# A two-layer graph kernel: weight rows over 128 partitions, a reordered start, and A h2 ahead of the last products

## Chip, cores and metric

The kernel runs on one core of a Trainium2 chip. The metric is the device time of one execution in microseconds (us), taken as the median of several runs; lower is better. The profile is one more execution, recorded by the hardware profiler; its own span is 2327.0 us.

## The reference

128 graphs of 128 nodes with 512 features. Layer 0 is a diffusion with an attention-weighted transition matrix; layer 1 is a linear attention over the adjacency matrix. Both take the layer norm and relu of their input and add to it. All is float32. In both, B = 128, N = 128, D = 512:

```
h  = relu(layernorm(x))
Xw = h @ Wv0 + bv
e  = leaky_relu(Xw @ aw[:d] (per column) + Xw @ aw[d:] (per row) + ab, 0.2)
T  = adj * exp(e), each row divided by its sum
x  = x + relu(h @ Wk[0] + bk[0] + T h @ Wk[1] + bk[1] + T T h @ Wk[2] + bk[2])

h2 = relu(layernorm(x))
q, k = split(h2 @ Wqk);  v = h2 @ Wv1
w  = (1 / sqrt(512)) * mask * rowsum(q * (adj @ (k * mask)))
x  = x + softmax over the nodes(w) * v
```

## The kernel before, in words

**Tiling.** Two graphs make a pair (p = 0 to 63), and one pair is worked on at a time. Nodes lie on the 128 partitions. The weights stay in SBUF for the whole run.

**The algebra.** Xw is never formed. `attention_columns` (L175) multiplies Wv0 by the two attention vectors into one extra column for each half of Wk[2], so that one product h [Wk[2] | column] gives Y2 and the attention terms together (257 columns for each half). T is then applied in two steps: Y10 + T (Y1 + T Y2), called `inner` (L426) and `outer` (L436). In layer 1 the score q * (A k) is computed as h2 M * (A h2) with M = Wq Wk^T, one 512x512 "score matrix" made at the start by `score_matrix` (L224) in four steps f = 0 to 3, so that one product h2 [M | Wv1] gives both the score side and v. A h2 is made by `aggregate` (L448), one 128x512 product for each graph.

**Strassen.** The products of a pair (2 graphs by 2 halves of the columns) use 7 block products in place of 8 (`strassen`, L306). It needs sums of the left side (`left_sums`, L294, on VectorE) and of the right side (`combine`, L156, on VectorE, once for each weight: `right2` for Y2, `right10` for Y10, `rightl` for layer 1). The seven products are issued in the order 1, 5, 6, 2, 7, 3, 4 into four PSUM banks a, e, b, c, with ScalarE copies between banks. There are two sets of banks: set 1 (a1, b1, c1, e1) for Y10, `inner`, `outer` and the score matrix; set 2 (a2, b2, c2, e2) for Y2 and layer 1. The argument `steps` lets other work be issued after a given product.

**Setup.** The input DMAs are issued by SP: x of pair 0 (L78), Wqk in four tiles (L117), Wv0, Wk[2], x of pair 1, Wk[1] and Wk[0] (all through `rows`, L136), later the adjacency (L84) and Wv1. `rows` permutes the rows of a weight: for each c it loads 32 partitions, each with four row pieces. Small constants come through the queues of ScalarE (L118) and GpSimd (L119 to L123). TensorE then transposes Wqk (`weights_transposed`, L209, eight groups of four transposes, each followed by a ScalarE copy) and h of pair 0 (`transposed_by_pe`, L286). The attention vectors are spread over the partitions by two products with a row of ones (L178) and two ScalarE copies (L179).

**Order.** Each engine works through its own queue in order. A scheduler sets the order of the queues from the order in which the code issues the work; `tc.issue_after(x)` says that what is issued within it stands after instruction x, and `behind` is a short form of that. In the loop, pair p runs Y10(p), the transpose of T (`t_transposed`, L395), `inner`, Y2 of pair p + 1, `outer`, then layer 1 of pair p - 1, and on the other engines the norm and transposes of the pairs ahead (`norm0`, `begin`, `norm2`, `attention`). For the transposes of h on VectorE, h goes to DRAM (`hd`) and comes back in blocks (`hv`). For pairs 0 and 1 the attention column is spread over the partitions by two TensorE transposes (`spread`, L152), for later pairs by DMA through GpSimd's queue. `seed` (L404) copies the bias into banks a1 and e1, into which Y10 accumulates.

**The end.** After the last pair's layer 0 only layer 1 of pair 63 remains (`layer1` with `last`). There, graph 0's A h2 follows product 3, its score and softmax follow at once (`score`, L499; `finish_graph`, L493), and graph 1's A h2 follows product 4. `end22` also finishes pair 62 (L538 scales its v and adds it to x).

Of the kernel before, what the change touches and what calls it, by code (L numbers as in the profile page):

```python
# [8 lines left out]
FP = mybir.dt.float32  # L9
# [6 lines left out]
def kernel(  # L16
# [30 lines left out]
    G = 2  # L47
# [19 lines left out]
                                      ("a1", "b1", "c1", "e1", "a2", "b2", "c2", "e2"))  # L67
    set1, set2 = (a1, b1, c1, e1), (a2, b2, c2, e2)

    def bcast(ap, offset, n):  # L70

        return bass.AP(tensor=ap.tensor, offset=ap.offset + offset, ap=[[0, P], [1, n]])
# [33 lines left out]
    wkt = setup.tile([P, DC, D], FP, name="wkt")  # L106
    aw_bc = setup.tile([P, 2, D], FP, name="aw_bc")
    awr = t10[0:1, 2].rearrange("p c o -> p (c o)")
    bkr = t10[:K, 3, 0]
    nm = setup.tile([B, N], FP, name="nm")  # L110
    ab_bc = setup.tile([P, 1], FP, name="ab_bc")
    awc = setup.tile([P, 2, DC], FP, name="awc")
# [22 lines left out]

    def rows(dst, w):  # L136

        for c in range(DC):
            nc.sync.dma_start(dst[c * S32:(c + 1) * S32],
                              w[c * P:(c + 1) * P].rearrange("(f a) o -> a f o", a=S32))  # L140

    def rows_by_halves(dst, w):
        for nh in range(2):
# [28 lines left out]
    maskT = const.tile([P, B], FP, name="maskT")  # L172
    wscale = const.tile([P, B], FP, name="wscale")

    def attention_columns():  # L175

        for a, bank in enumerate((b2, c2)):
            nc.tensor.matmul(bank, ones[0:1, :], awr[:, a * D:(a + 1) * D], start=True, stop=True)  # L178
            nc.scalar.copy(aw_bc[:, a, :], bank)  # L179
        for f in range(DC):  # L180
            for a in range(2):
                junk = front.tile([P, D], FP, name="junk", bufs=1)
                nc.vector.scalar_tensor_tensor(junk, wv0_sb[:, f], 1.0, aw_bc[:, a, :], op0=OP.mult,
                                               op1=OP.mult, accum_out=r2[:, f, a, HD:W2])

    def attention_constant():

        ccol = small.tile([P, 2], FP, name="ccol", bufs=1)
        for a in range(2):
            nc.vector.scalar_tensor_tensor(awc[:, a], awc[:, a], 1.0, bvc, op0=OP.mult,  # L190
                                           op1=OP.mult, accum_out=ccol[:, a:a + 1])
        for a in range(2):
            nc.tensor.matmul(e2[:, 0:1], ones, ccol[:, a:a + 1], start=(a == 0), stop=(a == 1))
        nc.vector.tensor_add(cz, e2[:, 0:1], ab_bc)

    def masks():

        nc.tensor.transpose(a2[:, :B], nm, ident[:B, :B])
        nc.scalar.copy(maskT, a2[:, :B])
        nc.scalar.activation(wscale, maskT, AF.Copy, scale=float(D) ** -0.5)  # L200

    def bias():


        nc.tensor.matmul(b2, ones[:K, :], bkr, start=True, stop=True)
        nc.scalar.copy(bias_a[:, 1], b2[:, :HD])
        nc.vector.tensor_sub(bias_e[:, 1], b2[:, HD:], bias_a[:, 1])

    def weights_transposed():  # L209

        banks = [a2, e2, a1, b1, c1, e1]
        for c in range(DC):
            for a in range(2):
                bank = banks[(c * 2 + a) % len(banks)]
                pt = bank.rearrange("p (o i) -> p o i", o=DC)
                for o in range(DC):
                    at = a * D + o * P
                    nc.tensor.transpose(pt[:, o, :], wqk_sb[:, c, at:at + P], ident)
                if a:
                    nc.scalar.copy(wkt[:, :, c * P:(c + 1) * P], pt)  # L220
                else:
                    nc.scalar.copy(wqt[:, :, :, c, :], pt.rearrange("p o (f a) -> p o f a", f=Q))

    def score_matrix(f):  # L224

        bank = set1[f]
        for o in range(DC):
            nc.tensor.matmul(bank, wqt[:, o, f].rearrange("p c a -> p (c a)"), wkt[:, o],
                             start=(o == 0), stop=(o == DC - 1))
        nc.scalar.copy(rl[:, f, :, 0, :], bank.rearrange("p (h o) -> p h o", h=2))  # L230


# [73 lines left out]
    def strassen(banks, left, right, s, first, ends, steps={}):  # L306

        w = right[1].shape[-1]  # L310
        a, b, c, e = (t[:, :w] for t in banks)

        def product(bank, i, start=False):
            for k in range(HC):
                nc.tensor.matmul(bank, left[i][:, k * P:(k + 1) * P], right[i][:, k],  # L315
                                 start=(start and k == 0), stop=(k == HC - 1),
                                 skip_group_check=True)
            if i in steps:
                steps[i]()

        product(a, 1, first)
        nc.scalar.copy(b, a)  # L322
        product(e, 5, first)
        nc.scalar.copy(s[:, 0], e)  # L324
        product(b, 6)
        done["u2"] = nc.scalar.copy(c, b).ins  # L326
        product(a, 2)
        ends[0, 0](a)
        product(c, 7)
        nc.scalar.copy(s[:, 1], c)  # L330
        ends[1, 1](e, s[:, 1])
        product(b, 3)
        ends[0, 1](b, s[:, 0])
        product(c, 4)
        ends[1, 0](c)
# [11 lines left out]
    def y2(p):  # L347

        y = Y2[p] = front.tile([P, G, 2, WP], FP, name="y2")[:, :, :, :W2]
        s = front.tile([P, 2, WP], FP, name="s2", bufs=1)[:, :, :W2]  # L350
        strassen(set2, LEFT[p], right2, s, True, {
            (0, 0): lambda a: nc.scalar.copy(y[:, 0, 0], a),
            (1, 1): lambda e, t: nc.vector.tensor_add(y[:, 1, 1], e, t),  # L353
            (0, 1): lambda b, t: nc.vector.tensor_add(y[:, 0, 1], b, t),
            (1, 0): lambda c: nc.scalar.copy(y[:, 1, 0], c)})
        if p > 1:

            t = small.tile([P, G, S32], FP, name="pzt", bufs=1)
            nc.vector.transpose(t, y[:, :, 0, W2 - S32:])  # L359
            d = dram.tile([G, Q, S32], FP, name="pzd")  # L360
            nc.gpsimd.dma_start(d.rearrange("g q b -> q g b"), t[S32 - 1::S32])  # L361
            PZ[p] = front.tile([P, G, N], FP, name="pz", bufs=1)
            nc.gpsimd.dma_start(PZ[p].rearrange("p g n -> p (g n)"), bcast(d, 0, G * N))
        else:
            PZ[p] = a2[:, :G * N].rearrange("p (g n) -> p g n", g=G)
            for j in range(G):
                spread(PZ[p][:, j, :], y[:, j, 0, HD:])
        return s

    def attention(p, room):  # L370

# [29 lines left out]
        nc.scalar.copy(tt, pt)  # L401
        TT[p] = tt

    def seed():  # L404

        nc.scalar.copy(a1, bias_a.rearrange("p k o -> p (k o)"))
        nc.scalar.copy(e1, bias_e.rearrange("p k o -> p (k o)"))

    blocks1 = [(0, 0, a1), (1, 1, e1), (0, 1, b1), (1, 0, c1)]

    def behind(what, op, *args):

        with tc.issue_after(done[what]):
            return op(*args)

    def y10(p, steps):

# [37 lines left out]
    def layer1(p, steps={}):  # L455
# [10 lines left out]

        def end12(b, t):
            nc.vector.tensor_add(o[0, 1], b, t)
            aggregate(p, 0, a2)
            if last:  # L470
                score(p, yv, w, a2, 0)
                finish_graph(p, yv, w, 0, b1)

        def end22(e, t):
            nc.vector.tensor_add(o[1, 1], e, t)
            if last:
                end(t[:, :G])

        strassen(set2, LEFT2.pop(p), rightl, s, True, {
            (0, 0): lambda a: nc.scalar.copy(o[0, 0], a),  # L480
            (1, 1): end22,
            (0, 1): end12,
            (1, 0): lambda c: nc.scalar.copy(o[1, 0], c)}, steps)
        aggregate(p, 1, e2)
        if last:
            score(p, yv, w, e2, 1)
            finish_graph(p, yv, w, 1, c1)
        else:
            score(p, yv, w, a2, 0)
            score(p, yv, w, e2, 1)  # L490
        return yv, w, s
# [54 lines left out]
            finish(peak, *ends.pop())  # L546


    h0 = norm_relu(xg[0], "h", front, True)
    weights_transposed()  # L550
    hT0 = front.tile([P, G, DC, N], FP, name="x")
    transposed_by_pe(h0, hT0, (a2, e2))
    attention_columns()
    attention_constant()
    bias()
    LEFT[0] = left_sums(hT0, front, "sx", 2)
    score_matrix(0)
    score_matrix(1)
    masks()
    right2 = combine(halves(r2), [t2[:, i] for i in range(4)])  # L560
    with tc.issue_after(done["right"]):
        norm0(1)
    right10 = combine(halves(r10), [t10[:, i] for i in range(4)])
    with tc.issue_after(done["right"]), tc.issue_after(done["hv"]):
        for p in range(2):
            load_adj(p)
        y2(0)
        attention(0, front.tile([P, D], FP, name="junk", bufs=1)[:, :G * N])
        load_x(2)
        load_adj(2)  # L570
        rows_by_halves(rl[:, :, :, 1, :], wv1)
    score_matrix(2)
    score_matrix(3)
    seed()

    HV2 = {}
    for p in range(NP + 1):
# [5 lines left out]
        if p < NP:  # L583
# [10 lines left out]
                transposed(HV2.pop(p - 1), X2)  # L594
                LEFT2[p - 1] = left_sums(X2, late["p"], "sx2", 1)

            s0 = y10(p, {1: lefts, 6: lambda: t_transposed(p)})
            z = inner(p)
            s2 = y2(p + 1) if p + 1 < NP else s0
            end(s2[:, 0, :G])  # L600
            outer(p, z)
            if p == 0:
                setup_ctx.close()
                late["p"] = ctx.enter_context(tc.tile_pool(name="late", bufs=1))
            if p + 1 < NP:
                seed()
            if p == 0:
                norm2()
            if p + 3 < NP:
# [46 lines left out]
```

## Time and profile before

| what | value |
|---|---|
| median of 3 runs | 2328.38 us (2328.36 to 2328.64) |
| span of the profiled execution | 2327.0 us |
| TensorE (PE) busy | 2304.2 us, 99% |
| VectorE (DVE) busy | 1361.0 us, 58% |
| ScalarE (ACT) busy | 1028.8 us, 44% |
| GpSimd (POOL) busy | 336.6 us, 14% |
| mean granted clock of PE | 0.999 |
| share of the chain that ended last on PE | 98% |
| DMA | 241.55 MB, mean 104 GB/s; SP's and ACT's queue 29.9% of the 16 DMA engines' time, GpSimd's 5.1% |

PE is TensorE's matmuls, PEld its weight loads, SP the engine that issues most DMAs. "L218" is line 218 of the kernel before. A float32 product of a 128x512 tile appears as two MATMUL records of 0.43 us each when the clock is up, so "x8" is four products. A transpose is one record. In the tile names the buffer and bank numbers are left out: "a" is a1 or a2, "t" can be t2, t10 or the T of the attention. "[7.14 <-ACT aw_bc L179]" says that the engine stood idle for 7.14 us before this instruction, until ACT had written aw_bc at L179. The granted clock in the tables is the throttle's, not the start-up state of PE; that one shows in the durations.

### The profile page before, as it was taken

The numbers are of one execution on the slowest core, as the hardware profiler recorded it, in microseconds if no ns is written. First come the engines' busy times: TensorE is split into PE (matmuls) and PEld (weight loads), VectorE is DVE, ScalarE is ACT, GpSimd is POOL, SyncE is SP. The second block draws the span as 40 slices with busy tenths as digits, with TensorE's granted clock in tenths as the row PEclk, the third lists the DMA queues.
The fourth block names the chain that finished last, engine by engine and source line by source line (L and its number), as shares of the span: only waits on it lengthen the run. The fifth ranks groups of instructions, "written<-read, shape, count | busy, mean of one in ns | idle before, by whom it ended". The sixth has DMA issues, their size and how long they took to land.

```text
span 2327.0 us, 23621 instructions
## 1 busy us (share of the span) xinstructions
PE 2304.2 (99%) x6881; PEld 1290.7 (55%) x6881; DVE 1361.0 (58%) x4131; ACT 1028.8 (44%) x2517; POOL 336.6 (14%) x585
## 2 busy tenths in 40 slices
PE   7999999999999999999999999999999999999998
PEld 4555555555555555555555555555555555555554
DVE  3656566556556565565665665665656655656654
ACT  3444444444444444444444444444444444444443
POOL 2111111111111111111111111111111111111100
PEclk9999999999999999999999999999999999999999
DMA  7433333333333333333333333333333333333321
GB/s 171 113 105 98 121 89 106 111 98 109 103 102 110 105 97 114 97 98 114 95 109 110 99 108 103 98 114 105 90 118 91 108 111 98 109 102 99 109 64 50
DMA packets 249860, 241.55 MB, mean 104 GB/s; under 512 B 26062, under 2 KB 175566, under 8 KB 249730
## 3 DMA queue, kind: packets, MB, share of 16 engines
q1 hardware_dynamic: 229360, 215.01, 29.9%
q0 software_dynamic: 20368, 25.03, 5.1%
q8 instruction: 54, 0.88, 0.2%
q14 instruction: 76, 0.62, 0.1%
q10 hardware_dynamic: 2, 0.00, 0.0%
HBM read 140.20 MB, written 99.74 MB: 103 GB/s over the span
## 4 chain that ended last, share of the span: by engine, by line
PE 98%; ACT 1%; DVE 0%; DMA 0%; issue 0%; POOL 0%; DVEq 0%; ACTq 0%; POOLq 0%
PE a L315 24%; PE c L315 24%; PE b L315 24%; PE e L315 12%; PE a L453 2%; PE e L453 2%; PE a L431 1%; PE c L431 1%; PE c L441 1%; PE b L441 1%; PE e L431 1%; PE e L441 1%; PE b L431 1%; PE a L441 1%; PE a L400 1%; ACT h L257 0%
## 5 line engine op out<-in xcount | busy, mean ns | idle before, releaser
L315 PE MATMUL a<-r,x 128*128 128x257 f32 (+1 forms) x1024 | 373.1, 486 | 1.4 <-ACT b L322 1.4
L88 POOL DMA_DIRECT2D agb<-in_adj_dram x256 | 152.2, 599 | 844.7 <-DVE t L386 783.2
L353 DVE TENSOR_TENSOR y<-e,s 128x257 f32<-128x257 f32 x64 | 27.3, 427 | 403.8 <-ACT s L330 403.8
L315 PEld LDWEIGHTS a<-r,x 128*128 128x128 f32 x1024 | 189.3, 190 | 107.3 <-issue 91.2
L315 PE MATMUL a<-rl,x 128*128 128x512 f32 x512 | 240.7, 592 | 1.4 <-issue 1.4
L330 ACT COPY s<-c 128x512 f32<-128x512 f32 (+1 forms) x192 | 97.8, 510 | 209.5 <-PE c L315 209.4
L315 PE MATMUL c<-t,sx 128*128 128x257 f32 (+1 forms) x512 | 186.6, 487 | 1.2 <-ACT c L326 1.1
L315 PE MATMUL c<-t,x 128*128 128x257 f32 (+1 forms) x512 | 186.3, 486 | 0.3 <-ACT s L330 0.3
L315 PE MATMUL e<-t,sx 128*128 128x257 f32 (+1 forms) x512 | 186.4, 486 | 0.0
L315 PE MATMUL b<-t,sx 128*128 128x257 f32 (+1 forms) x512 | 186.2, 486 | 0.0
L315 PE MATMUL b<-r,sx 128*128 128x257 f32 (+1 forms) x512 | 186.2, 486 | 0.0
L361 POOL DMA_DIRECT2D pzd<-pzt x62 | 36.9, 595 | 951.5 <-DVE pzt L359 905.9
L326 ACT COPY c<-b 128x512 f32<-128x512 f32 (+1 forms) x192 | 95.8, 499 | 177.4 <-PE b L315 177.4
L324 ACT COPY s<-e 128x512 f32<-128x512 f32 (+1 forms) x192 | 98.8, 515 | 161.8 <-PE e L315 161.7
L283 DVE STREAM_TRANSPOSE x<-hv 128x512 f32<-128x512 f32 x252 | 163.5, 686 | 6.1 <-DMA hv<-hd 6.0
L315 PEld LDWEIGHTS a<-rl,x 128*128 128x128 f32 x512 | 97.2, 190 | 96.9 <-issue 93.6
L246 DVE TENSOR_TENSOR r<-r 128x2 f32<-128x2 f32 x128 | 20.0, 156 | 211.1 <-ACT r L245 210.9
L322 ACT COPY b<-a 128x512 f32<-128x512 f32 (+1 forms) x192 | 96.1, 500 | 97.7 <-PE a L315 89.7
L315 PEld LDWEIGHTS c<-t,sx 128*128 128x128 f32 x512 | 96.9, 190 | 70.6 <-issue 60.5
L315 PEld LDWEIGHTS c<-t,x 128*128 128x128 f32 x512 | 97.2, 190 | 68.7 <-issue 61.2
L315 PEld LDWEIGHTS b<-r,sx 128*128 128x128 f32 x512 | 97.3, 190 | 68.1 <-issue 61.2
L315 PEld LDWEIGHTS b<-t,sx 128*128 128x128 f32 x512 | 97.3, 190 | 68.1 <-issue 45.9
(205 smaller groups left out, 3910.2 us busy)
## 6 DMA issues: line engine op xcount, KB each, us to landing
hd<-h SPq DMA_DIRECT2D x126, 512.0 KB, 2.8
hv<-hd SPq DMA_DIRECT2D x504, 128.0 KB, 2.9
xg<-in_x_dram SPq DMA_DIRECT2D x64, 512.0 KB, 3.9
out_dram<-x SPq DMA_DIRECT2D x63, 512.0 KB, 4.3
agb<-in_adj_dram POOLq DMA_DIRECT2D x256, 32.0 KB, 2.1
ag<-in_adj_dram SPq DMA_DIRECT2D x64, 128.0 KB, 2.6
pw<-pwd POOLq DMA_DIRECT2D x63, 128.0 KB, 3.4
pz<-pzd POOLq DMA_DIRECT2D x62, 128.0 KB, 3.7
```

The lines of the kernel that those rows point to most:

```text
L88: nc.gpsimd.dma_start(agb[p][c * S32:(c + 1) * S32].rearrange("p g q i -> p (g q) i"), v[c])
L283: nc.vector.transpose(dst[:, j].rearrange("p f (n b) -> p f n b", n=Q), hv[:, j].rearrange("p n (f a) -> p f n a", f=Q))
L315: nc.tensor.matmul(bank, left[i][:, k * P:(k + 1) * P], right[i][:, k], start=(start and k == 0), stop=(k == HC - 1), skip_group_check=True)
L322: nc.scalar.copy(b, a)
L324: nc.scalar.copy(s[:, 0], e)
L326: done["u2"] = nc.scalar.copy(c, b).ins
L330: nc.scalar.copy(s[:, 1], c)
L353: (1, 1): lambda e, t: nc.vector.tensor_add(y[:, 1, 1], e, t),
L361: nc.gpsimd.dma_start(d.rearrange("g q b -> q g b"), t[S32 - 1::S32])
L431: nc.tensor.matmul(bank[:, :HD], TT[p][:, j, :], y[:, j, nh, :HD], start=False, stop=True, skip_group_check=True)
L441: nc.tensor.matmul(bank[:, HD:], tt[:, j, :], z[:, j, nh], start=False, stop=True, skip_group_check=True)
L453: nc.tensor.matmul(to, AT[p][:, j, :], h2, start=True, stop=True)
```

## The change

1. `rows` loads each weight in four DMAs over all 128 partitions, one row piece for each partition, in place of four DMAs over 32 partitions with four pieces each. Bytes, number of DMAs and placement in SBUF stay.
2. The bias rows `bkr` get a tile of their own (they lay in t10), and the small setup products use other banks (e1, c1).
3. Four products of `ones` with itself (`warm(4)`) stand first on TensorE, then the two attention vectors (`attention_vectors`, split off), then six more (`warm(6)`); the norm of pair 0 and the transposes of Wqk come behind them. Half of the copies after Wqk's transposes go to VectorE.
4. Three steps of the score matrix stand ahead of Y2 of pair 0, the fourth behind it; `combine` for `right10`, and `attention(0)`, come ahead of `norm0(1)`; the adjacency of pairs 0 and 1 is loaded ahead of h's way through DRAM. `seed` is split into `seed_a` and `seed_e`; the spreading of the attention column is split off Y2 (`spread_columns`).
5. In the loop, `t_transposed` is issued behind product 6, and pair 1's attention column is spread right after Y2 of pair 1.
6. In layer 1 of the last pair, both A h2 products come after product 1, into a1 and e1, ahead of products 5, 6, 2, 7, 3 and 4. Half of graph 1's score is computed early (after product 7, from the right half of e1), the other half straight from bank c after product 4, with the left half of A h2 copied to SBUF by ScalarE, and the two are added.

```diff
     def rows(dst, w):
 
-        for c in range(DC):
-            nc.sync.dma_start(dst[c * S32:(c + 1) * S32],
-                              w[c * P:(c + 1) * P].rearrange("(f a) o -> a f o", a=S32))
+        for f in range(Q):
+            nc.sync.dma_start(dst[:, f], w.rearrange("(c f a) o -> f c a o", c=DC, f=Q)[f])
...
                 if a:
-                    nc.scalar.copy(wkt[:, :, c * P:(c + 1) * P], pt)
+                    done["wkt"] = nc.vector.tensor_copy(wkt[:, :, c * P:(c + 1) * P], pt).ins
...
         def end12(b, t):
             nc.vector.tensor_add(o[0, 1], b, t)
-            aggregate(p, 0, a2)
             if last:
-                score(p, yv, w, a2, 0)
+                score(p, yv, w, a1, 0)
                 finish_graph(p, yv, w, 0, b1)
+            else:
+                aggregate(p, 0, a2)
 
         def end22(e, t):
             nc.vector.tensor_add(o[1, 1], e, t)
             if last:
                 end(t[:, :G])
+                half_score(e1[:, HD:], yv[:, 1, 1, 0, :], 3)
+
+        def half_score(y, agg, at):
+            junk = front.tile([P, D], FP, name="junk", bufs=1)
+            nc.vector.scalar_tensor_tensor(junk[:, :HD], y, wscale[:, B - 1:B], agg, op0=OP.mult,
+                                           op1=OP.mult, accum_out=w[:, at:at + 1])
+
+        def end21(c):
+            nc.scalar.copy(o[1, 0], c)
+            if last:
+                half_score(c[:, :HD], agg, 1)
+                nc.vector.tensor_add(w[:, 1:2], w[:, 1:2], w[:, 3:4])
+                finish_graph(p, yv, w, 1, c1)
+
+        if last:
+            agg = front.tile([P, G, 2, HD], FP, name="zz", bufs=1)[:, 0, 0]
+            steps = {1: lambda: (aggregate(p, 0, a1), aggregate(p, 1, e1),
+                                 nc.scalar.copy(agg, e1[:, :HD]))}
...
-    h0 = norm_relu(xg[0], "h", front, True)
-    weights_transposed()
+    warm(4)
+    attention_vectors()
+    with tc.issue_after(done["aw"]):
+        h0 = norm_relu(xg[0], "h", front, True)
+    behind("vector", warm, 6)
+    with tc.issue_after(done["warm"]):
+        weights_transposed()
     hT0 = front.tile([P, G, DC, N], FP, name="x")
     transposed_by_pe(h0, hT0, (a2, e2))
-    attention_columns()
-    attention_constant()
-    bias()
     LEFT[0] = left_sums(hT0, front, "sx", 2)
-    score_matrix(0)
-    score_matrix(1)
-    masks()
-    right2 = combine(halves(r2), [t2[:, i] for i in range(4)])
-    with tc.issue_after(done["right"]):
-        norm0(1)
-    right10 = combine(halves(r10), [t10[:, i] for i in range(4)])
-    with tc.issue_after(done["right"]), tc.issue_after(done["hv"]):
+    masks()
+    behind("wkt", attention_constant)
+    bias()
+    with tc.issue_after(done["left"]):
+        attention_columns()
+        right2 = combine(halves(r2), [t2[:, i] for i in range(4)])
+    for f in range(Q - 1):
+        score_matrix(f)
+    with tc.issue_after(done["right"]):
+        right10 = combine(halves(r10), [t10[:, i] for i in range(4)])
+    with tc.issue_after(done["right"]), tc.issue_after(done["m"]):
+        y2(0)
+        seed_a()
+        spread_columns(0)
+        score_matrix(Q - 1)
+        seed_e()
         for p in range(2):
             load_adj(p)
-        y2(0)
         attention(0, front.tile([P, D], FP, name="junk", bufs=1)[:, :G * N])
+        norm0(1)
+    with tc.issue_after(done["hv"]):
         load_x(2)
         load_adj(2)
         rows_by_halves(rl[:, :, :, 1, :], wv1)
-    score_matrix(2)
-    score_matrix(3)
-    seed()
...
-            s0 = y10(p, {1: lefts, 6: lambda: t_transposed(p)})
+            s0 = y10(p, {1: lefts, 6: lambda: behind("product", t_transposed, p)})
```

## The prediction, made before the result was known

> **What bounds it now.** I read the busy time by stage first, cut where the work changes: to pair 0's Y10, to pair 2's Y10, the loop, the last pair's end (columns: stretch, PE, PEld, DVE, ACT, POOL busy, clock, DMA share, GB/s).
>
> ```profile
> 0.00:48.00 48.00, 34.91 (x114) 20.27 (x114) 17.30 (x53) 17.54 (x35) 9.04 (x24) 1.00 0.69 161
> 48.00:111.00 63.00, 59.49 (x184) 33.27 (x184) 41.60 (x115) 27.99 (x65) 8.09 (x14) 1.00 0.48 123
> 111.00:2305.00 2194.00, 2193.94 (x6550) 1230.54 (x6549) 1292.60 (x3938) 977.04 (x2400) 317.83 (x544) 1.00 0.34 103
> 2305.00:2327.00 22.00, 15.82 (x38) 6.65 (x36) 9.52 (x29) 6.25 (x18) 1.67 (x3) 0.95 0.17 54
> ```
>
> PE never rests from 111 to 2305, and there the change leaves every queue's order as it was. All that can move lies in the first 111 us and the last 22. Next PE's timeline (start, duration, engine, line, the wait before it):
>
> ```profile
> 4.26 1.91 PE L178 MATMUL c<-t,ones 1*128 1x512 f32 x2
> 13.30 2.07 PE L205 MATMUL b<-t,ones 3*128 3x512 f32 x2 [7.14 <-ACT aw_bc L179]
> 15.30 1.11 PE L218 MATMUL a<-ident,tl 128*128 128x128 f32 x4
> 21.00 0.60 PE L218 MATMUL e<-ident,tl 128*128 128x128 f32 x4
> 33.95 3.60 PE L228 MATMUL e<-wkt,wqt 128*128 128x512 f32 x8
> 37.38 1.03 PE L315 MATMUL a<-r,x 128*128 128x257 f32 x4
> 47.76 0.32 PE L154 MATMUL a<-ident,y 128*128 128x128 f32 x1 [1.63 <-ACT y L355]
> 47.97 1.95 PE L315 MATMUL a<-r,x 128*128 128x512 f32 x4
> ```
>
> PE stands 7.14 us behind two ACT copies, which stand behind h0, whose statistics stand on DVE behind a small product waiting for awc (landed 7.8). Four transposes take 1.11 us cold and 0.60 once the clock is up, near 20.7. Y2 starts at 37.38. Then the loads, by stretch, in the same columns:
>
> ```profile
> 4.00:6.00 2.00, 2.00 (x3) 0.33 (x1) 0.00 (x0) 0.00 (x0) 2.00 (x9) 1.00 1.02 405
> 15.00:20.00 5.00, 5.00 (x23) 4.70 (x23) 0.42 (x1) 2.85 (x6) 0.00 (x0) 1.00 1.09 212
> 25.00:30.00 5.00, 5.00 (x13) 2.13 (x13) 4.79 (x14) 1.18 (x2) 0.00 (x0) 1.00 1.09 200
> ```
>
> With the engines full, x and Wqk (128 partitions) run at 405 GB/s, the row loads (32) at 200 to 212. Last, DVE at the end:
>
> ```profile
> 2316.99 0.69 DVE L468 TENSOR_TENSOR t<-b,s 128x512 f32<-128x512 f32 x1
> 2317.85 0.75 DVE L503 SCALAR_TENSOR_TENSOR junk<-a,wscale,t 128x512 f32<-128x512 f32 x1
> 2318.99 1.41 DVE L538 SCALAR_TENSOR_TENSOR x<-yv,wcol,x 128x512 f32<-128x512 f32 x2
> 2320.32 0.28 DVE L525 TENSOR_REDUCE peak<-b 128x1 f32<-128x128 f32 x1
> 2320.61 0.75 DVE L503 SCALAR_TENSOR_TENSOR junk<-e,wscale,t 128x512 f32<-128x512 f32 x1
> 2323.30 0.75 DVE L538 SCALAR_TENSOR_TENSOR x<-t,wcol,x 128x512 f32<-128x512 f32 x1
> ```
>
> From product 3's end (2316.96) DVE has hardly a gap until 2322: DVE, as much as PE, sets the end.
>
> **What the Trainium skill says.** "SBUF — State Buffer", section "Door 1: The DMA port swizzle": a DMA's bandwidth follows how many of 16 SBUF ports its partitions reach; by its table, 32 aligned partitions reach 8. The trace agrees: 200 to 212 against 405. "DMA: Bandwidth & Descriptors", "Specifications": pieces of 512 B or more suffice for line rate; here they stay 1 and 2 KB. "TensorE: Matmul & The Clock Gate", Part 1: the clock doubles after some 3.4 us of sustained work, on a free-running window. The trace agrees in kind: 3.75 us of work at 2.4 did not do it, 7.4 us from 13.3 did. Part 4 there doubts that transposes count; here it rose during transposes.
>
> **The front, step by step.** My times are estimates from this profile's durations, each queue taken in its new order.
>
> Start: four warm products from 1.05 (`ones` ready), two L178 products, six warm: a cold 128x512 costs 1.84 (2.42 to 4.26), so 128 columns 0.46; 10 x 0.46 + 2 x 1.84 = 8.3, to 9.4. They cost nothing: Wqk's first tile landed at 6.4, and x plus Wqk, 2.6 MB at 0.405 MB/us from about 2.3, is in by 9. ACT: the two copies end at 7.1, and from L244 to the end of h0 took 3.16, so h0 is ready at 10.3. The moved awc product (0.25 on DVE) now hides behind Wqk's copies.
> Transposes: 8 groups at 0.43 warm = 3.4, to 12.9; the copies are split, four on ACT (0.49 apart), four on DVE (0.61), which ends the one-engine line. Mask 0.1, bias 0.86, h0 0.9, two tiny ones 0.2: the score matrix starts at 15.0 (was 22.83).
> Three steps of 3.43: 25.3. DVE needs the h0 copy and four sums to about 17.3, 8 L183 at 0.73 = 5.8 and four combinations 2.6: 25.7. Y2 takes these one at a time, the last 5 us into Y2. No wait. The data: after Wqk come 4.7 MB, at 405 GB/s 11.6 us, to 20.6. The lower bound for 128 partitions is the page's own mix, 104 GB/s at a share of 35.3%, so 295 when full, its 512-byte pieces included: 15.9, to 25. right10 is needed at 26. I take 340; 295 costs under 1 us.
> Y2 with all ready: 14 x 0.434 = 6.1 instead of 10.4; two spreads 0.2, step four 3.4, and about 0.5 waiting for ACT's last Y2 copy. Y10 of pair 0 starts at 35.5 (was 47.97): 12.5 gained.
>
> What is moved behind: norm0(1) now follows attention(0). Its relu on ACT waits for rs, which on DVE stands behind attention's products, which wait for ACT's Exp: to about 36.7. Behind it on ACT stand 0.71 + 0.49 + 0.71 + 0.49 (relu, last rl copy, relu, seed of e1), and PE's product 5 waits for that seed: 39.2 against 37.3, so 2 us lost. Bounds: 0 if DVE is a microsecond early, 4 if late. On SP, hd and hv of pair 1 leave at 39 behind adj (before 47.5), so `begin(1)` (DVE, after Y10) and the Wv1 rows behind them are early too. POOL's queue is unchanged. Between the two Y10 the products sum to 57.5 us of the 63.0; the 5.5 are waits and refills. After: 57.5 + 2 + 0.9 for three small ones + 1.1 for refills that adding up misses = 61.5. Pair 2's Y10 at 97.0 (was 110.93): **13.9 gained**. The copies of `t_transposed` behind "product" and the split seed move nothing in the loop.
>
> **The tail, step by step.** No product is saved but its place: the two A h2 products (0.86 each) go ahead of products 5 to 3, so product 3 ends 2 x 0.86 = 1.72 later, at 2318.7. DVE's chain hangs from there: before, L468 to the last L538's start took 6.3. After: the half score of e1 (0.44 + 0.1) stands ahead of the sum, 0.55 late; sum 0.65; score 0.75; scale 0.3; two L538 1.3; reduce 0.2; half score 0.45; 0.5 until Exp's sum is in; three small ones 0.3; L538 of graph 0 0.7 (now ahead of graph 1's reduce); reduce, Exp, reciprocal, product 1.4: 7.1, so its start is 2325.8 (was 2323.30). Allowing for overlaps I take **2.2 lost**; bounds 3.0 lost, and 0.5 gained if pair 62's scaling (two L538) did not stand in the chain, which it does.
>
> Sum: -13.9 + 2.2 = -11.7; I allow 0.3 more for the clock: span 2315.6. The runs' median is 1.4 above the span of 2327.0 (2328.38), so **2317.0 us**.
>
> **Rivals.** That the change doesn't do what it says is none: on the changed queues three steps do precede Y2, and A h2 the products. (1) The clock comes up late. For: a free window, and only transposes between 9.4 and 15. Against: ten products without a break. From 9.4 to 15 cold costs 2.6, up to 20 about 4.7: 2319.6 to 2321.7; with the ACT wait at 4, 2323.7.
> (2) Loads gain nothing: 1 KB pieces at 205 GB/s. Then right10's rows land at 38 as before, DVE's combinations of them stand ahead of Y2's sums, the gain of the front shrinks to about 2 and the tail takes it: 2328. Against: the 405 and the 295.
> (3) Slower: one DMA now walks 128 scattered 1 KB rows of the weight; should that run below about 200, say 190, the last rows come at 41, pair 0's Y10 follows, and with the tail's 2.2 it ends near 2332. It decides from some 205 down. For: no load of this form is in the trace.
>
> **Chances.** Forecast 0.76, its own range 2313.5 to 2321.5 (fast clock and no ACT wait at the low end; late clock or 280 GB/s at the high); a late clock with a long ACT wait, 2321.5 to 2323.7, 0.13; (2) 0.07; (3) 0.04. A measurement of this kernel tells 0.2% (4.7 us) from no change. Faster 0.89, same 0.07, slower 0.04. Range 2313.5 to 2322.
>
> **What would show it.** Row loads at 300 or more with the share near 1; four transposes at 0.6 from the start; first L228-type product near 15, Y2 near 25, Y10 near 35.5, then one wait of about 2 us on ACT's seed of e1; pair 2's Y10 at 97. In the tail, product 4 ending 14.6 us after pair 62's last A h2 began (2305.80), the last L538-type 20.4 after it (was 18.25). Row loads at 200, or a tail no longer than before, would prove me wrong there.

## The result, and the profile after

The changed kernel takes **2347.49 us** (median of 4 runs, 2347.26 to 2348.93), against 2328.51 us for the kernel before in the same runs (2328.36 to 2329.06): a ratio of 1.0082, with a 95% interval from 1.0065 to 1.0100. It is slower by 19 us. The prediction said 2317.0 and faster.

The profiled execution after has a span of 2347.2 us (2327.0 before). Line numbers from here on are those of the changed kernel: L144 are the row loads (L139 before), L231 the transposes of Wqk (L218), L241 the score matrix (L228), L328 the products (L315), L466 A h2 (L453), L567 the scaling (L538).

Busy time by stage, after; the stages are cut at the same pieces of work as before, so their limits have moved (columns: stretch, PE, PEld, DVE, ACT, POOL busy, granted clock, DMA share, GB/s):

```profile
0.00:48.00 48.00, 37.00 (x126) 23.41 (x126) 16.06 (x46) 12.39 (x24) 9.05 (x24) 0.93 0.43 139
48.00:129.00 81.00, 62.98 (x190) 35.95 (x191) 44.95 (x125) 31.30 (x72) 8.09 (x14) 0.87 0.40 112
129.00:2325.00 2196.00, 2195.76 (x6554) 1231.21 (x6553) 1294.50 (x3941) 977.62 (x2401) 317.78 (x544) 1.00 0.35 102
2325.00:2347.00 22.00, 14.05 (x34) 5.93 (x32) 8.48 (x28) 5.99 (x18) 1.68 (x3) 0.91 0.16 54
```

The loop is as full as before. The loss lies ahead of 129, where PE stands idle for 29 us of the 129 (16.6 of the first 111 before). The DMA share in the first 48 us has fallen from 0.69 to 0.43, although the same bytes have to come in. PE's timeline of the start (start, duration, engine, line, the wait before it):

```profile
9.66 1.06 PE L231 MATMUL a<-ident,tl 128*128 128x128 f32 x4
11.95 0.60 PE L231 MATMUL b<-ident,tl 128*128 128x128 f32 x4
15.42 0.63 PE L231 MATMUL a<-ident,tl 128*128 128x128 f32 x4 [1.03 <-DMA tl<-in_L_gnn_Wqk_dram]
19.22 3.68 PE L241 MATMUL a<-wkt,wqt 128*128 128x512 f32 x8
35.31 1.88 PE L328 MATMUL e<-t,sx 128*128 128x257 f32 x4 [4.68 <-DVE t L163]
65.64 0.48 PE L158 MATMUL a<-ident,y 128*128 128x128 f32 x1 [19.77 <-ACT y L368]
70.37 1.88 PE L328 MATMUL a<-r,x 128*128 128x512 f32 x4
```

The score matrix does start earlier (19.22, was 22.83), and so does Y2 (29.60, was 37.38). But then PE waits 4.68 us for a sum of right2 (DVE L163) and 19.77 us for one ACT copy, and Y10 of pair 0 starts at 70.37 (was 47.97). The ACT copy stood in ACT's queue behind an instruction that waited for DVE, whose timeline shows what DVE waited for:

```profile
57.83 1.23 DVE L163 TENSOR_TENSOR t<-r 128x1024 f32<-128x1024 f32 x1 [18.44 <-DMA r<-in_L_gnn_Wk_dram]
60.63 1.23 DVE L165 TENSOR_TENSOR t<-r 128x1024 f32<-128x1024 f32 x1 [1.57 <-DMA r<-in_L_gnn_Wk_dram]
```

The last rows of Wk landed at 60.6. The load stretches, in the columns of the first table:

```profile
4.00:6.00 2.00, 2.00 (x4) 0.66 (x2) 0.91 (x2) 0.58 (x1) 2.00 (x9) 1.00 1.13 350
15.00:20.00 5.00, 4.45 (x25) 3.00 (x26) 2.10 (x10) 2.08 (x5) 0.00 (x0) 1.00 0.28 103
25.00:30.00 5.00, 5.00 (x14) 2.34 (x13) 0.03 (x2) 0.78 (x2) 0.00 (x0) 1.00 0.27 93
```

The row loads run at about 100 GB/s with a share of about **a quarter**: half the rate of before (200 to 212 at a share of 1.09), and without filling the engines. SP's own timeline says that nothing else was in the way. It issues row loads without a break from 4.00 to 53.96, with only x of pair 1 between them (before: from 3.27 to 34.39, with gaps). It looks as if each issue now waited for room in the queue, but that is not shown:

```profile
4.00 6.42 SPq L144 DMA_DIRECT2D t<-in_L_gnn_Wv_dram  x4
10.46 19.20 SPq L144 DMA_DIRECT2D r<-in_L_gnn_Wk_dram  x8
29.70 1.78 SPq L83 DMA_DIRECT2D xg<-in_x_dram  x1
31.53 22.43 SPq L144 DMA_DIRECT2D r<-in_L_gnn_Wk_dram  x16
```

The 24 loads of Wk take SP a median of 1.27 us each (0.31 before); 131 KB in 1.27 us is 103 GB/s, the rate of the transfers. The chain of work that ended last, by engine, has SP's queue in it, with 2% of the span:

```profile
PE 96%; SPq 2%; DVE 0%; ACT 0%; DMA 0%; issue 0%; ACTq 0%; DVEq 0%
```

At the end, DVE's timeline:

```profile
2337.19 0.69 DVE L481 TENSOR_TENSOR t<-b,s 128x512 f32<-128x512 f32 x1
2338.78 1.41 DVE L567 SCALAR_TENSOR_TENSOR x<-yv,wcol,x 128x512 f32<-128x512 f32 x2
2343.44 0.75 DVE L567 SCALAR_TENSOR_TENSOR x<-t,wcol,x 128x512 f32<-128x512 f32 x1
```

Pair 62's last A h2 began at 2323.68, so the last scaling ends 20.51 us after it (18.41 before). The whole difference in four pieces:

| piece | before | after | difference |
|---|---|---|---|
| start to Y10 of pair 2 | 110.93 | 128.79 | +17.86 |
| from there to pair 62's last A h2 | 2194.71 | 2194.89 | +0.18 |
| from there to the end of the last scaling | 18.41 | 20.51 | +2.10 |
| from there to the end of the span | 2.95 | 3.01 | +0.06 |
| sum | 2327.0 | 2347.2 | +20.2 |

The profiled execution is the longest of the four (2348.93 us), so its difference is 1.2 us more than that of the medians.

### The profile page after: what moved, and what is told of

It is laid out like the page before. It is cut to its first block, busy times and chain, and to the rows that moved or that the text cites. A ratio compares the mean times of both kernels' runs of the same rounds, so it can differ in the third digit from the quotient of the medians.

```text
span 2347.2 us, 23658 instructions
## 1 busy us (share of the span) xinstructions
PE 2309.8 (98%) x6901; PEld 1296.5 (55%) x6901; DVE 1364.0 (58%) x4138; ACT 1027.3 (44%) x2514; POOL 336.6 (14%) x585
## 4 chain that ended last, share of the span: by engine, by line
PE 96%; SPq 2%; DVE 0%; ACT 0%; DMA 0%; issue 0%; ACTq 0%; DVEq 0%
PE b L328 23%; PE c L328 23%; PE a L328 23%; PE e L328 12%; PE a L466 2%; PE e L466 2%; SPq L144 2%; PE b L454 1%; PE a L444 1%; PE c L444 1%; PE c L454 1%; PE e L454 1%; PE b L444 1%; PE e L444 1%; PE a L454 1%; PE a L415 1%
## 5 line engine op out<-in xcount | busy, mean ns | idle before, releaser
L328 PE MATMUL a<-r,x 128*128 128x257 f32 (+1 forms) x1024 | 373.6, 487 | 0.0
L328 PEld LDWEIGHTS a<-r,x 128*128 128x128 f32 x1024 | 190.1, 191 | 105.7 <-issue 91.9
L328 PE MATMUL a<-rl,x 128*128 128x512 f32 x512 | 240.6, 592 | 0.0
L328 PE MATMUL e<-t,sx 128*128 128x257 f32 (+1 forms) x512 | 187.2, 488 | 4.8 <-DVE t L163 4.7
L328 PE MATMUL b<-t,sx 128*128 128x257 f32 (+1 forms) x512 | 187.3, 489 | 1.4 <-DVE t L164 1.1
L328 PE MATMUL c<-t,x 128*128 128x257 f32 (+1 forms) x512 | 186.3, 486 | 0.2 <-ACT s L343 0.2
L328 PE MATMUL c<-t,sx 128*128 128x257 f32 (+1 forms) x512 | 186.5, 487 | 0.0
L328 PE MATMUL b<-r,sx 128*128 128x257 f32 (+1 forms) x512 | 186.4, 486 | 0.0
L328 PEld LDWEIGHTS a<-rl,x 128*128 128x128 f32 x512 | 97.3, 190 | 95.1 <-issue 91.8
L328 PEld LDWEIGHTS e<-t,sx 128*128 128x128 f32 x512 | 97.4, 191 | 73.7 <-issue 60.7
L328 PEld LDWEIGHTS b<-t,sx 128*128 128x128 f32 x512 | 97.6, 191 | 70.6 <-issue 46.2
L328 PEld LDWEIGHTS c<-t,sx 128*128 128x128 f32 x512 | 97.6, 191 | 68.3 <-issue 61.0
L328 PEld LDWEIGHTS c<-t,x 128*128 128x128 f32 x512 | 97.2, 190 | 68.6 <-issue 61.2
```

Source lines behind the costliest of these rows:

```text
L328: done["product"] = nc.tensor.matmul(bank, left[i][:, k * P:(k + 1) * P], right[i][:, k], start=(start and k == 0), stop=(k == HC - 1), sk ...
```

## The experiments

**Theory.** The prediction looked at where a row load arrives (128 partitions in place of 32) and not at how it is cut up. "DMA: Bandwidth & Descriptors" in the Trainium skill says under "Why a DMA increments its semaphore by 16 and not by 1", for the number k of engines, that the slowest dimension of each side is taken, and that it "picks the largest k ≤ 16 that divides both of those dim sizes". The new source pattern has the 4 blocks outermost (`f c a o`, c = 4), so k would be 4. My estimate from that: 4 engines of 16, a share of 0.25, and a quarter of the 405 GB/s of x and Wqk. Rival A: rows scattered over the weight, or a pattern with one dimension more, are slow in themselves. Rival B: the reordering of the queues costs the time.

**The order of two source dimensions.** This leaves destination, sizes, rows and number of the loads, and the order of every queue, as in the changed kernel. Rows land on other partitions, so it measures the loads and is no usable kernel:

```diff
-            nc.sync.dma_start(dst[:, f], w.rearrange("(c f a) o -> f c a o", c=DC, f=Q)[f])
+            nc.sync.dma_start(dst[:, f], w.rearrange("(c f a) o -> f a c o", c=DC, f=Q)[f])
```

> The changed kernel, only with the two row dimensions of the source exchanged in the row loads: the 32 rows of a block outermost, the 4 blocks inside, instead of the 4 blocks outermost. The same 128 rows of 1 KB go to the same 128 partitions in as many DMAs; rows land on other partitions, so the weights' rows are permuted wrongly and the output is not the reference's. Theory (the outermost dimension of 4 lets a DMA use only 4 of the 16 engines: share 0.25, 100 GB/s): with 32 outermost all 16 work, the row loads show a share near 1 and 350 to 400 GB/s, SP's issue of one falls from 1.27 us to about 0.4, Y2 starts near 25, pair 2's Y10 near 98, time 2315 to 2320. Rival A (scattered 1 KB rows or a fourth dimension cost the time, in DRAM or in making the descriptors): nothing changes, 95 to 105 GB/s, 2345 to 2349. Rival B (the new order of the queues costs the time): the loads may get faster, but the time stays above 2335.

Measured: 2319.31 us (2319.17 to 2319.98), ratio to before 0.9961 (0.9946 to 0.9976), 28 us faster than the changed kernel. Two stretches of its trace that hold row loads (of the first one's 266 GB/s, 32 are GpSimd's):

```profile
15.00:18.00 3.00, 3.00 (x16) 1.73 (x15) 1.50 (x9) 1.17 (x3) 0.00 (x0) 1.00 1.09 266
25.00:30.00 5.00, 5.00 (x19) 3.27 (x18) 2.60 (x5) 1.32 (x3) 0.00 (x0) 1.00 0.70 202
```

SP's row loads by duration (minimum, median, maximum in ns):

```profile
L144 SPq DMA_DIRECT2D r<-in_L_gnn_Wk_dram x24: 534/602/602, 6.3 to 28.7; - x24
```

and PE's longest wait of the start:

```profile
36.84 0.32 PE L158 MATMUL a<-ident,y 128*128 128x128 f32 x1 [2.06 <-ACT y L368]
```

Both rivals fall: the same rows are as scattered as before, and the queues stand in the new order. Two sizes of the expectation were off: while the engines are full (share 1.04 to 1.09, from 9 to 18 us) all queues together move 266 to 325 GB/s, the last of Wqk among them at first, not 350 to 400; and the issue takes 0.60 us, not 0.4. After 19 us it is the issue that paces them: 131 KB every 0.64 us is 205 GB/s.

**Eight outermost.** A third point between 4 and 32, with rows further apart than in the changed kernel:

```diff
-            nc.sync.dma_start(dst[:, f], w.rearrange("(c f a) o -> f c a o", c=DC, f=Q)[f])
+            nc.sync.dma_start(dst[:, f], w.rearrange("(a f e) o -> f e a o", e=8, f=Q)[f])
```

> The changed kernel with the source of each row load written as 8 groups of 16 rows, the 8 outermost (every 32nd row inside a group): 128 rows of 1 KB over 128 partitions in as many DMAs, every queue in the same order. Rows land on other partitions and the rows taken are others, so the output is not the reference's. Theory (the outermost number of the source sets how many engines work): 8 engines at 25 GB/s, so a share of 0.5 and about 200 GB/s in the stretches that hold only row loads (0.25 and 100 with 4, 0.9 to 1.05 and 270 to 300 with 32); SP's issue is not far above the 0.60 us of the run with 32; time 2317 to 2326. Rival A (scatter of the rows): these rows lie further apart than those of the changed kernel, so 100 GB/s or less and 2345 or more.

Measured: 2327.08 us (2326.08 to 2328.21), ratio 0.9992 (0.9983 to 1.0001). A stretch that holds nothing but row loads, and PE's wait, in this kernel's windows and timeline:

```profile
25.00:30.00 5.00, 5.00 (x18) 3.21 (x17) 3.97 (x10) 1.33 (x4) 0.00 (x0) 1.00 0.54 189
```

```profile
43.35 0.47 PE L158 MATMUL a<-ident,y 128*128 128x128 f32 x1 [8.49 <-ACT y L368]
43.61 5.19 PE L241 MATMUL e<-wkt,wqt 128*128 128x512 f32 x6
```

Rate and share are as the theory has them: 4 and 8 outermost give 93 to 103 and 189 to 196 GB/s, at shares of 0.26 to 0.28 and 0.54; with 32 the share is about 1, as full engines show it (1.04 to 1.09). The traces also hold the packets of every DMA (the pieces in which it moves its data), with start and duration. On SP's queue, 4 packets are in flight at once for 78% of the time and 5 for nearly all of the rest in the changed kernel (20 to 25 us), 8 or 9 for 92% of the time with 8 outermost (25 to 30), and a mean of 15 with 32 (15 to 18). A packet of 1 KB takes 46 ns with 4 and with 8 outermost, against about 87 in the kernel before (25 to 30), which had a mean of 17 in flight. So the gain that the prediction hoped for is there in each packet, but only a quarter as many run at once. The time is 1 us above the range that I gave; the wait of 8.49 us was followed by products at half speed: six records took 5.19 us here and 2.74 in the run with 32.

**The old row loads in the changed kernel.**

```diff
-        for f in range(Q):
-            nc.sync.dma_start(dst[:, f], w.rearrange("(c f a) o -> f c a o", c=DC, f=Q)[f])
+        for c in range(DC):
+            nc.sync.dma_start(dst[c * S32:(c + 1) * S32],
+                              w[c * P:(c + 1) * P].rearrange("(f a) o -> a f o", a=S32))
```

> The changed kernel with the row loads of the kernel before (32 partitions, four 1 KB pieces each); everything else of the change stays. Theory (the new row loads are the whole loss): 200 to 210 GB/s as before, right10's rows land near 34, time 2322 to 2329, faster than or equal to before. Rival B (the new order costs): stays above 2335.

Measured: 2329.77 us (2328.68 to 2333.06), ratio 1.0006 (0.9998 to 1.0015), 0.8 us above the range that I gave. The row loads are back at 209 GB/s (15 to 20 us) and Y10 of pair 0 starts at 40.29, 7.7 us earlier than before, yet nothing of it is left at the end: Y10 of pair 2 starts at 110.09, 0.8 us earlier than before. This is not a clean reversal: though only the loads were edited, the scheduler put other instructions into another order too, and pair 1's h now comes behind products of pair 0. It leaves SBUF at 56.27 (42.41 in the run with 32 outermost), and PE's timeline shows the price:

```profile
64.52 2.08 PE L329 MATMUL a<-r,x 128*128 128x257 f32 x4 [5.97 <-DVE x L297]
```

With the 2.1 us of the end, the early start is used up. So without the new row loads the loss is gone, but the reordering, as the scheduler carried it out here, gains nothing at the old rate.

**The new row loads in the kernel before.** The same edit the other way round.

> The kernel before with the new row loads and nothing else of the change. Theory: 100 GB/s, the last rows land near 58 to 60, Y10 of pair 0 starts near 65 to 70 instead of 47.97, time 2343 to 2350. Rival B (the new order costs, the slow loads are hidden): 2328 to 2333.

Measured: 2347.33 us (2346.66 to 2347.82), ratio 1.0080 (1.0063 to 1.0097). The loads alone make the whole loss; rival B has nothing left. Y10 of pair 0 starts at 55.86, not at 65 to 70 as I expected, but then waits for its seed:

```profile
67.47 3.78 PE L314 MATMUL e<-t,sx 128*128 128x512 f32 x4 [9.73 <-ACT e L406]
```

Here too the scheduler moved some instructions; a run below separates that from the rate.

**The end alone.** The kernel before with part 6 of the change.

> The kernel before with only the change of the last pair: both A h2 ahead of the products, graph 1's score in halves. All else, the queues' order until the last pair too, as before. Theory (from the two traces: the last scaling ended 20.5 us after pair 62's last A h2 began, 18.4 before): 2.1 us slower, 2330.2 to 2331.0. Rival (the end is limited by the products, and A h2 ahead takes its own 0.86 us from behind the last product): 0.5 to 1 us faster, 2327.5 to 2328.

Measured: 2330.96 us (2330.39 to 2331.91), ratio 1.0009 (1.0001 to 1.0017). Its last DVE lines:

```profile
2321.14 1.41 DVE L554 SCALAR_TENSOR_TENSOR x<-yv,wcol,x 128x512 f32<-128x512 f32 x2
2325.80 0.75 DVE L554 SCALAR_TENSOR_TENSOR x<-t,wcol,x 128x512 f32<-128x512 f32 x1
```

Pair 62's last A h2 began at 2306.04, the scaling ends 20.51 us later: 2.10 more than before, the same as in the changed kernel.

**A complete version on all engines.** For layer 0 the permutation moves from the weights' rows to h, which ScalarE writes anyway. Piece f of a weight is then 128 rows that lie together, with 128 outermost. Wv1 keeps the loads of the kernel before. The core of it:

```diff
-            nc.sync.dma_start(dst[:, f], w.rearrange("(c f a) o -> f c a o", c=DC, f=Q)[f])
+            nc.sync.dma_start(dst[:, f], w[f * P:(f + 1) * P])
...
+            if name == "h" and permuted:
+                to, at = (to.rearrange("p (c f a) -> p c f a", c=DC, f=Q),
+                          at.rearrange("p (f c a) -> p c f a", c=DC, f=Q))
```

> A complete version of the changed kernel whose loads use all engines: the rows of Wv0 and Wk stay in their natural order (piece f of a load is rows 128 f to 128 f + 127, one outermost dimension of 128), and the permutation moves to h of layer 0, which ScalarE writes in permuted column order as it already did for pair 0; pair 0's h is no longer permuted. Wv1 keeps the loads of the kernel before. Theory: like the run with 32 outermost (2319.3), or up to 2 us better if rows that lie together load faster: 2316.5 to 2320.5. Rival A (scatter matters too): clearly better than 2317. What could be against it: a permuted write of h costs ScalarE more than 0.81 us for 128x512 in the loop; nothing there waits for it.

Measured: 2318.68 us (2317.99 to 2319.32), ratio 0.9955 (0.9940 to 0.9970): 0.6 us better than scattered rows with 32 outermost, with ranges that overlap, and with SP's issue down to a median of 0.43 us.

**One DMA for each half, and the old end.** The lines of the end, as in the kernel before, are left out here:

```diff
-        for f in range(Q):
-            nc.sync.dma_start(dst[:, f], w[f * P:(f + 1) * P])
+        nc.sync.dma_start(dst, w.rearrange("(f p) o -> p f o", p=P))
```

> The version with natural rows, with one DMA of four pieces for each half of a weight in place of four, and the last pair's end as in the kernel before. In the run with 32 outermost SP's issue took 0.60 us for each 128 KB, so no more than 210 GB/s after 19 us, and DVE waited 2.67 us for the last rows. Theory: with a quarter of the issues the last rows land 1 to 3 us earlier, and the old end gives back 2.1 us: 2313.5 to 2316.5. If the issue was not the limit: 2316.5 to 2318. If the end did not cost anything, no better than the version with natural rows.

Measured: 2317.07 us (2316.25 to 2317.39), ratio 0.9948 (0.9936 to 0.9961), 0.6 us above the range expected and inside the one for an issue that was no limit. With six issues in place of 24 for Wk the row loads, at last, fill the engines (x of pair 1 is among them in the first stretch):

```profile
15.00:20.00 5.00, 5.00 (x18) 2.56 (x18) 3.56 (x10) 0.87 (x2) 0.00 (x0) 1.00 1.08 316
20.00:25.00 5.00, 5.00 (x13) 2.13 (x12) 4.83 (x14) 1.76 (x3) 0.00 (x0) 1.00 1.09 353
```

Y10 of pair 2 starts at 97.52 (99.17 with four DMAs), and the last scaling ends 18.42 us after pair 62's last A h2. That is 3.7 us together; the medians differ by 1.6. Of the rest, 0.7 is the stretch from the last scaling to the end of the span, 3.68 us in place of 2.93; why it grew stays open. The other 1.4 comes from the executions profiled: the slowest of its four there, the fastest of its five here. So the time alone does not show what the fewer issues are worth.

**Without the ten products of ones.** The version with natural rows and four DMAs, all queues otherwise in the same order.

```diff
-    warm(4)
...
-    behind("vector", warm, 6)
-    with tc.issue_after(done["warm"]):
+    with tc.issue_after(done["vector"]):
         weights_transposed()
```

> The version with natural rows (2318.7) without the ten products of ones at the start; every queue keeps its order otherwise. Theory as in the prediction (the ten products fill time in which TensorE waits anyway and bring the clock up earlier): with them four transposes fell to 0.60 us by 11.1; without them the clock starts at the two attention products near 3 and the transposes begin when the first tile of Wqk and the copies allow, near 7 to 9.5; 8 groups cold instead of 2 cost up to 6 x 0.42 = 2.5 us, so 2318.7 to 2321.2. Rival (they only delay the transposes, which could start at 7 and warm the clock themselves): 2317 to 2318.5.

Measured: 2318.26 us (2317.95 to 2318.88), ratio 0.9956 (0.9942 to 0.9969): no different from the 2318.68 with them, below the range of my theory and in the rival's. The first transposes then start at 6.38 instead of 9.52; the last two groups, behind a wait for Wqk, are cold again:

```profile
13.01 1.08 PE L237 MATMUL a<-ident,tl 128*128 128x128 f32 x4 [0.94 <-DMA tl<-in_L_gnn_Wqk_dram]
```

**Natural rows alone in the kernel before.** This has the queues of the run with the new loads alone (but for ACT's copies of two steps), and so separates the rate from the order.

> The kernel before with nothing but the natural row order of Wv0 and Wk (16 engines, 128 partitions, permuted h of layer 0); the scheduler then gives the queues the same order as in the run of the kernel before with the changed row loads (2347.3), apart from ACT's copies of two steps, so the two differ in the rate of the loads. Theory A (most of the gain of the front comes from the loads): Y2 no longer waits between its products, 2318 to 2323. Theory B (the loads must come together with the new order): Y2 still starts near 37 and only its gaps go, 2324 to 2329.

Measured: 2320.25 us (2319.55 to 2321.05), ratio 0.9963 (0.9950 to 0.9977). In nearly one order, loads at 100 GB/s give 2347.33 and loads at 192 to 335 (x and the last of Wqk included) give 2320.25: 27 us from the rate alone. Y2 starts at 29.55 and Y10 of pair 0 at 42.84. Theory A holds.

**Both ends of the sum.** First the changed kernel with natural rows, one DMA for each half, without the ten products, with the old end; then the kernel before with natural rows and one DMA for each half.

> What the runs so far point to: the changed kernel with natural rows, one DMA of four pieces for each half of a weight, without the ten products of ones, and with the last pair's end of the kernel before. Theory: the parts add up, so the run with the old end and the one DMA (2317.1) less the 0.4 us that leaving out the ten products gave: 2315.5 to 2317.5. Rival (the ten products matter once the loads come earlier): 2317.5 to 2320.

> The kernel before with natural rows of Wv0 and Wk and one DMA of four pieces for each half; nothing else of the change (the scheduler orders some instructions otherwise than with four DMAs). Theory A (with fast loads the start of the kernel before is bound by TensorE's late start at 13, not by the loads): no more than 1 us from the run with four DMAs, 2319.3 to 2321.3. Theory B (fewer issues also bring Y2 earlier): 2317 to 2319.

Measured: **2316.51 us** (2316.12 to 2316.57), ratio 0.9947 (0.9934 to 0.9959), and 2319.38 us (2318.99 to 2319.98), ratio 0.9960 (0.9947 to 0.9974). The first beats both kernels, by 12.2 and 31 us. Both times lie in the ranges that I gave. Of the 12.2 us, 9.3 come with the loads alone, 2.9 with the rest of the change, less the ten products and the new end.

## Why the prediction was wrong, step by step

**The step that failed is the price of the row loads.** The prediction took 340 GB/s and called 295 "the lower bound for 128 partitions"; they ran at 93 to 103. The last rows, put at 20.6 to 25, landed at 60.6. "No wait" for the sums of right2 became 4.68 us, and the wait for ACT's last Y2 copy, put at 0.5, became 19.77. Both rates were carried over from x, Wqk and the page's average, that is in the main from transfers whose outermost dimension is 128 or 32; the DMA whose price was wanted has 4 outermost. No load of that form is in the trace before, as the prediction itself said under its third rival. So 295 was no bound from below: it left out how many engines a DMA runs on. The limit that the prediction took from "SBUF — State Buffer", section "Door 1: The DMA port swizzle", held (a 1 KB packet took 46 ns with 128 partitions and about 87 with 32), and its 340 was near the rate of full engines (353 GB/s with one DMA for each half), but the number of engines is another limit. What the runs show is that rate, share and packets in flight go with the outermost number of the source: twice as much with 8 as with 4, and full engines with 32. This fits the skill's rule; the trace does not name single engines, and the destination had 128 outermost in all of these runs, so that side of the rule was not tried.

**Rival 3 had the right direction, mechanism and size wrong.** It named one DMA over 128 scattered rows, at 190 GB/s and near 2332. The scatter costs little: the same rows with 32 outermost gave 2319.31, and rows lying together 2318.68. The rate was half of 190. Its size is off for its own rate too: the run with 8 outermost had 189 to 196 GB/s and took 2327.08, not 2332.

**Rival 2 was nearly right about its own case.** It said that at 205 GB/s the gain goes and 2328 remains, since right10's rows land at 38 and DVE's combinations of them stand ahead of Y2's sums. In the run with 8 outermost, which has the new order and nearly that rate, these combinations start at 36.88, Y2's first sum follows them at 42.23, and the time is 2327.08. So the chain from a slow load to the end was right; the rate that went into the forecast was wrong. That it came so close is in part luck, as the half speed after the wait of 8.49 us was not in the sum.

**The front, at the rate I had meant.** The run with 32 outermost tests the other steps:

| step | predicted | measured there |
|---|---|---|
| transposes of Wqk begin | 9.4 | 9.52 |
| score matrix begins | 15.0 | 17.20 |
| Y2 begins | 25.3 | 27.58 |
| seven products of Y2 | 6.1 | 6.07 |
| wait for ACT's last Y2 copy | 0.5 | 2.06 |
| Y10 of pair 0 | 35.5 | 39.58 |
| wait for ACT's seed of e1 | 2.0 | 1.46 |
| Y10 of pair 2 | 97.0 | 99.30 |
| time | 2317.0 | 2319.31 |

Three terms were too small. First, the clock: with the ten products done, three groups of transposes were still cold (1.06 us), and 0.60 came only near 12.5. That costs 3 x 0.43 = 1.3 us and is half of rival 1. PE had then been busy from 1.09 on, some 11 us (10 in the version with natural rows), so the 3.4 us of sustained work that the prediction took over did not hold here. Second, the small setup products and pair 0's h, put at 2.06 us between the transposes and the score matrix, take 2.9 (14.30 to 17.20). Third, the wait for ACT's last Y2 copy: ACT stands behind DVE's combinations of right10, and their rows, paced by SP's issue, came only at 30.3 (needed at 26, by the prediction). That the ten products "cost nothing" holds, but they bring nothing either. The two Y10 lie 59.7 apart, not 61.5, which gave 1.8 us back.

**The tail was right, in its steps too.** Predicted 2.2 lost; 2.10 in the trace of the changed kernel and of the end alone. From pair 62's last A h2, product 3 ends 1.72 us later than before, as predicted; the half score delays DVE's next sum by 0.44 (0.55 predicted); from that sum to the last scaling it takes 6.25 in place of 6.31. (From product 3 to the last scaling that is 6.72; the prediction added up 7.1 and allowed for overlaps.) The last scaling ends 20.5 us after that A h2 (20.4 predicted). The prediction counted from 2305.80, where PE's timeline has 2305.64, hence its 18.25 and the 18.41 of the table above.

**The chances.** 0.04 for slower was too little for a form of transfer that no trace had shown, since the whole front hung on its price.

## What to carry to other kernels

Price a DMA by its whole pattern on both sides: how many partitions it reaches, how many pieces it has, and which number stands outermost; a transfer with a 4 outermost ran at a quarter share here, and exchanging two dimensions was worth 28 us. Two signs told the limits apart here. With 4 outermost the share was a quarter while the issue of one load stretched to 0.69 to 6.84 us: the transfers were too narrow. With 32 the share was 0.70 (25 to 30 us) while each issue took the same 0.60 us, one behind the other: the issue was the limit. Where the price of a form is not in the trace and all the rest hangs on it, the bound from below has to include the worst that the form allows.

## What the runs showed that I had not expected

- SP's issue of a 131 KB load took 0.31 us for 32 partitions with four pieces, 0.43 for 128 rows lying together and 0.60 for 128 rows in a pattern of two dimensions (medians of the Wk loads before, with natural rows, and with 32 outermost).
- A waiting PE can lose its clock. After waits of 4.68 us (changed kernel), 5.97 us (old loads in it), 8.49 us (8 outermost) and 9.73 us (new loads in the kernel before) the next products took about twice their time: 1.88 us for four records of 257 columns that take 1.03, 3.78 for four of 512 that take 1.88. After a wait of 2.06 us (32 outermost) they did not. The granted clock shows it too, unlike at the start: it reads 0.50 from 36 to 42 and from 50 to 65 us in the changed kernel. The slow products there took some 4.9 us more than at full speed, an estimate from its durations (four products of Y2, 3.0 us; six records of the score matrix, 4.62 us in place of 2.74). So a long wait there costs more than its length. But length alone does not decide: in the run without the ten products, waits of 1.15 and 0.94 us were enough (0.50 from 14 to 16), and in the version of 2316.51 us waits of 0.74 and 0.94 at the same place were not.
- The shape of a DMA alone changed the order in which the scheduler put the other engines' queues; an experiment that swaps a load has to look at the order too.
